# An audio tower in written program order: tanh gate, deviation by a GpSimd power, layer-norm products on ScalarE, natural order of features, 314-column streams

## The chip, the cores and the metric

The kernel runs on one core of one Trainium2 chip. The metric is the device time in microseconds (us) of one execution. TensorE (PE in the profile) does the matmuls, VectorE (DVE), ScalarE (ACT) and GpSimd (POOL) the rest, SyncE (SP) issues most transfers. Every kernel here was run beside the kernel before on the same chip.

## The reference, cut to what matters

```python
frames = pad(x).reshape(64, 157, 512)             # 64 sequences of 157 tokens
h = frames @ dct.T                                # orthonormal DCT, 512 features
x = layernorm(h)
key_phase, query_phase = tanh(x @ Wk + bk) * pi, tanh(x @ Wq + bq) * pi
V = x @ Wv + bv
total = sum over sets and planes of the causal reads of V by phase   # "scores" x V
gate = sigmoid(x @ Wg + bg)
total = gate * total + (1 - gate) * sigmoid(posw) * (reads of V by position phases)
h = h + x + total / norm @ Wo + bo
y = layernorm(h)
e = argmax(mean over tokens(y) @ Wg2 + bg2)       # one of 16 experts for each sequence
h = h + softmax gate * (y @ We[e] + be[e])
```

All is float32. Four sequences make a group, so there are 16 groups. The 157 tokens of a sequence are a tile of 128 and a tail of 29; the tails of the four sequences share one fifth tile. Every tile is normalized twice, so a group has ten layer norms.

## The kernel before

The kernel is a pipeline over groups: while TensorE does the gate and the attention of one group, the frames of the next group are transformed, normalized and transposed. The order on each engine was left to a scheduler, which may move instructions. Some names for what follows: x is a tile after the first layer norm and x2 after the second; the residual (`res`) is h + x; PSUM is the memory that TensorE writes its results to, in a few tiles that are used in turn, so that a matmul can wait for a tile to be emptied; a transpose (on TensorE, then a copy by ScalarE) turns a tile for the next matmul; folding is the sums and differences of a frame that come before its transform; phasors are the sines of the phases; the router picks the expert. The parts that matter:

```python
def layernorm(x, h):
    ...                                            # bn_stats, bn_aggr on VectorE
    nc.scalar.activation(sd, mv[:, 1:2], AF.Sqrt, bias=eps)
    nc.vector.reciprocal(rstd, sd)
    nc.vector.tensor_scalar(x, h, mv[:, 0:1], rstd, ALU.subtract, ALU.mult)

# frames: four matmuls write a PSUM tile h in runs of 128 columns
quarter = h.rearrange("p (r j) -> p r j", r=4)
...
layernorm(x, h)
nc.vector.tensor_tensor(r, h, x, ALU.add)          # residual
nc.gpsimd.tensor_tensor(r, r, bo, ALU.add)

# gate: 512 columns for the tiles, then 116 for the tails; the trace has 77 table loads of 1.28 us at the sigmoid
moving = xT[:, c, HEADS] if k == 0 else by_tail(xT[:, c, TAILS])
nc.tensor.matmul(ps[:, k, :n], wg[:, c, o * P : (o + 1) * P], moving, ...)
nc.scalar.activation(gT[:, o, :, at], pb, AF.Sigmoid, bias=bg[:, o : o + 1])

# last step of an expert; the features are put back in order by a strided view
nc.vector.scalar_tensor_tensor(o.rearrange("p (j r) -> p r j", r=4), by_r(be), gate[:, m : m + 1], by_r(h), ...)
for i in range(GB):                                # the tail tile: four stores of 29 rows
    nc.sync.dma_start(out=out[GB * g + i, P:, :], in_=o[TL * i : TL * i + LT, :])
```

## Time and profile before

| | before |
|---|---|
| median (lowest to highest) | 1661.23 us (1660.85 to 1661.28) |
| span of the profiled run | 1659.1 us |
| TensorE, VectorE, ScalarE, GpSimd busy | 96, 56, 33, 20% |
| first output projection starts | 93.4 us |
| from one group's output projection to the next, steady | 100.5 us |
| last output projection starts | 1572.0 us |
| from there to the end of the span | 87.1 us |

TensorE is busy nearly all the time, so the span is a chain of TensorE's work with short waits in it. The start of a group's output projection (the 32 matmuls of `wo`) is a good milestone: it comes once in each group, and the differences between neighbours say what a group costs. The span is then three terms: the head (until the first of these starts), 15 steps between the 16, and the end.

### The profile page before, as it was taken

The page shows a single profiled execution, that of the slowest core. Times are in us where ns is not written, and L with a number is a line of the kernel's source. Part 1 is how long each engine was busy: PE and PEld are TensorE (multiplying, and loading weights), DVE is VectorE, ACT ScalarE, POOL GpSimd, SP SyncE. Part 2 cuts the span into 40 slices and gives each one's busy share as a digit, 9 for nine tenths or more (in the row PEclk, how much of TensorE's full clock was granted, in tenths as well). Part 3 has the DMA queues.
Part 4 walks back from the last instruction along what each step waited for, and adds up shares of the span by engine and source line. Part 5 has one row for each costly group of instructions (what it writes and reads, how often), then busy time and mean ns, then how long its engine had stood idle before and what let it go on. Part 6 is the DMA issues. An engine that isn't in the chain of part 4 may idle for free. (4 is left out here: it accounts for less than half of the span.)

```text
span 1659.1 us, 18042 instructions
## 1 busy us (share of the span) xinstructions
PE 1592.7 (96%) x6724; PEld 875.5 (53%) x6724; DVE 937.4 (56%) x2162; ACT 545.1 (33%) x769; POOL 326.6 (20%) x377
## 2 busy tenths in 40 slices
PE   7999999999999999999999999999999999999984
PEld 4555556464554645556454554645546455564531
DVE  6556647466463755747466474755637556464452
ACT  3634143251522515134250432515224251342110
POOL 3203112031120403103031120312104031030102
PEclk9999999999999999999999999999999999999997
DMA  5104113141211413013141121413114130121314
GB/s 188 32 1 146 31 56 110 51 146 45 104 48 51 146 48 136 25 45 140 51 146 36 64 97 51 146 45 116 36 51 146 49 136 18 36 112 51 114 50 164
DMA packets 41206, 135.40 MB, mean 82 GB/s; under 512 B 6224, under 2 KB 6624, under 8 KB 32544
## 3 DMA queue, kind: packets, MB, share of 16 engines
q0 software_dynamic: 15616, 88.09, 15.3%
q1 hardware_dynamic: 25504, 46.17, 8.2%
q8 instruction: 53, 0.87, 0.2%
q14 instruction: 33, 0.27, 0.0%
HBM read 113.67 MB, written 20.58 MB: 81 GB/s over the span
## 5 line engine op out<-in xcount | busy, mean ns | idle before, releaser
L306 PE MATMUL mm<-xT,wg 128*128 128x512 f32 (+1 forms) x1024 | 299.9, 438 | 10.0 <-DVE res L157 9.1
L131 PE MATMUL mm<-wv,xT 128*128 128x512 f32 x640 | 283.9, 598 | 3.6 <-ACT xT L111 3.6
L131 PE MATMUL mm<-we,x2T 128*128 128x512 f32 x512 | 225.2, 598 | 10.9 <-DMA we<-in_we,rows 10.9
L131 PE MATMUL mm<-wo,tT 128*128 128x512 f32 x512 | 222.3, 592 | 0.0
L306 PEld LDWEIGHTS mm<-xT,wg 128*128 128x128 f32 x1024 | 156.3, 192 | 114.0 <-issue 92.2
L131 PEld LDWEIGHTS mm<-wv,xT 128*128 128x128 f32 x640 | 119.4, 191 | 142.5 <-issue 137.2
L101 ACT ACT_TABLE_LOAD x93 | 119.3, 1283 | 215.7 <-DVE mv L99 213.5
L131 PEld LDWEIGHTS mm<-we,x2T 128*128 128x128 f32 x512 | 98.2, 192 | 134.3 <-issue 116.3
L119 POOL TENSOR_TENSOR odd<-frame 128x256 f32<-128x256 f32 x80 | 61.3, 767 | 501.2 <-issue 491.9
L131 PEld LDWEIGHTS mm<-wo,tT 128*128 128x128 f32 x512 | 97.3, 190 | 117.2 <-issue 111.0
L453 POOL DMA_INDIRECT be<-in_be,expi x80 | 76.4, 955 | 412.8 <-DVE o L476 404.8
L174 DVE TENSOR_TENSOR v<-mm,bv 128x512 f32<-128x512 f32 x80 | 55.4, 692 | 174.9 <-PE mm L131 174.9
L345 PE MATMUL mm<-att,v 128*128 128x314 f32 x512 | 149.1, 434 | 2.3
L111 ACT COPY x2T<-tr 128x512 f32<-128x512 f32 x80 | 43.7, 588 | 260.0 <-PE tr L110 243.5
L158 POOL TENSOR_TENSOR res<-res,bo 128x512 f32<-128x512 f32 x80 | 101.5, 1278 | 137.1 <-DVE res L157 121.6
L473 DVE TENSOR_TENSOR be<-mm,be 128x512 f32<-128x512 f32 x80 | 55.3, 692 | 126.2 <-PE mm L131 75.4
L101 ACT ACTIVATE sd<-mv,eps 128x1 f32<-128x1 f32 x160 | 47.2, 295 | 207.5 <-DVE mv L99 205.5
L345 PEld LDWEIGHTS mm<-att,v 128*128 128x128 f32 x512 | 92.5, 190 | 39.5 <-DVE att L326 5.7
L110 PE MATMUL tr<-ident,x 128*128 128x128 f32 x640 | 93.4, 277 | 16.4 <-DVE x L104 15.5
L110 PEld LDWEIGHTS tr<-ident,x 128*128 128x128 f32 x640 | 73.8, 141 | 59.1 <-DVE x L104 24.2
L311 ACT ACT_TABLE_LOAD x77 | 98.8, 1283 | 1.3
L476 DVE SCALAR_TENSOR_TENSOR o<-be,gate,res 128x512 f32<-128x512 f32 x80 | 92.9, 1162 | 4.8 <-DMA out<-o 2.0
(105 smaller groups left out, 1793.8 us busy)
## 6 DMA issues: line engine op xcount, KB each, us to landing
frame<-in_frames SPq DMA_DIRECT2D x80, 256.0 KB
out<-o SPq DMA_DIRECT2D x64, 256.0 KB
out<-o SPq DMA_DIRECT2D x64, 58.0 KB
be<-in_be,expi POOLq DMA_INDIRECT x80, 4.1
wv<-in_wv SPq DMA_DIRECT2D x1, 1024.0 KB
wg<-in_wg SPq DMA_DIRECT2D x1, 1024.0 KB
wo<-in_wo SPq DMA_DIRECT2D x1, 1024.0 KB
we<-in_we,rows POOLq DMA_INDIRECT x64, 8.7
```

The source lines that it names most:

```text
L101: nc.scalar.activation(sd, mv[:, 1:2], AF.Sqrt, bias=eps)
L110: nc.tensor.transpose(tr[:, c * P : (c + 1) * P], x[:, c * P : (c + 1) * P], ident)
L119: nc.gpsimd.tensor_tensor(odd, ft[:, :2, :], ft[:, 2:, :], ALU.subtract)
L131: nc.tensor.matmul(ps, lhs(c), w[:, c, :], start=(c == 0), stop=(c == C - 1))
L158: nc.gpsimd.tensor_tensor(r, r, bo, ALU.add)
L174: nc.vector.tensor_tensor(vt, ps, bv, ALU.add)
L306: nc.tensor.matmul(ps[:, k, :n], wg[:, c, o * P : (o + 1) * P], moving, start=(c == 0), stop=(c == C - 1))
L311: nc.scalar.activation(gT[:, o, :, at], pb, AF.Sigmoid, bias=bg[:, o : o + 1])
L345: nc.tensor.matmul(ps[:, c, : 2 * L], v[i][:, cols], att[i % 2], start=True, stop=True)
L453: nc.gpsimd.indirect_dma_start(out=be, out_offset=None, in_=a["be"], in_offset=bass.IndirectOffsetOnAxis(ap=expi[:, m : m + 1], axis=0),)
L473: nc.vector.tensor_tensor(be, ps, be, ALU.add)
L476: nc.vector.scalar_tensor_tensor(o.rearrange("p (j r) -> p r j", r=4), by_r(be), gate[:, m : m + 1], by_r(h), ALU.mult, ALU.add)
```

## The change

The intent: fewer and shorter streams on TensorE, no changes of ScalarE's tables within a stage (the trace before has 222 table loads of 1283 ns), work taken from VectorE, and an order in which each layer norm stands behind TensorE's work. (The gate's sigmoid becomes a tanh, since sigmoid(z) = (1 + tanh(z/2))/2; the sum with 1 and the half are put into the scores and the mask.) The core of the diff (most of it is the same work cut into functions that are then called in order):

```diff
+    ctx.enter_context(tc.manual_schedule())           # every engine in program order
...
-        nc.scalar.activation(sd, mv[:, 1:2], AF.Sqrt, bias=eps)
-        nc.vector.reciprocal(rstd, sd)
-        nc.vector.tensor_scalar(x, h, mv[:, 0:1], rstd, ALU.subtract, ALU.mult)
+        nc.gpsimd.tensor_scalar(rstd, mv[:, 1:2], EPS, None, ALU.add)
+        nc.gpsimd.tensor_tensor(rstd, rstd, power, ALU.pow)          # power = -0.5
+        nc.gpsimd.tensor_scalar(shift, mv[:, 0:1], rstd, -1.0, ALU.mult, ALU.mult)
...
+        nc.scalar.activation(x, h, AF.Identity, bias=shift, scale=rstd)
+        nc.scalar.activation(r, h, AF.Identity, bias=shift, scale=rstd1)   # x + h in one step
...
-            quarter = h.rearrange("p (r j) -> p r j", r=4)
+        by_r = h.rearrange("p (j r) -> p r j", r=4)   # natural order: every fourth column
...
-    moving = xT[:, c, HEADS] if k == 0 else by_tail(xT[:, c, TAILS])  # 512, then 116 columns
-    nc.scalar.activation(gT[:, o, :, at], pb, AF.Sigmoid, bias=bg[:, o : o + 1])
+    s["xT"][:, c, 2 * k : 2 * k + 2, :L]              # two sequences, 314 columns, twice
+    nc.scalar.activation(to, by_halves(ps), AF.Tanh, bias=hbg[:, o : o + 1], scale=0.5)
...
-                    nc.sync.dma_start(out=out[GB * g + i, P:, :], in_=o[TL * i : TL * i + LT, :])
+                for lo, hi in ((0, TL // 2), (TL // 2, LT)):            # 16 and 13 rows
+                    nc.sync.dma_start(out=out[GB * g + i, P + lo : P + hi, :], in_=o[TL * i + lo : TL * i + hi, :])
...
+    for g in range(NG):                               # the order, as written
+        project(g); route(g - 1); phasors(g); ...     # (calls put on one line here)
+        for m in range(NM):
+            embed(g + 1, m); turn(g + 1, m - 1); embed_ln(g + 1, m); load_frame(g + 2, m)
+            gate_part(g, m); scores(...)              # four gate parts, five frame tiles
+        read(g, 0); read_tails(g); turn(g + 1, NM - 1)
+        read(g, 1) ... read(g, 3); output(g, m) ...; expert(g - 1, m) ...
+        turn_x2(g)
```

## The prediction

> **What bounds the kernel now.** I read the page first, then the timeline of TensorE in one steady group of four sequences, then the end of the program, then the waits.
>
> ```profile
> span 1659.1 us, 18042 instructions
> PE 1592.7 (96%) x6724; PEld 875.5 (53%) x6724; DVE 937.4 (56%) x2162; ACT 545.1 (33%) x769; POOL 326.6 (20%) x377
> PE   7999999999999999999999999999999999999984
> ```
>
> TensorE is the bound from the second slice to the last but two; no other engine is above 56%. So only two things change the time: how long TensorE must stream, and the short gaps in its stream. The mean durations of the groups are no measure of streaming, because matmuls overlap: I take start to start in the timeline.
>
> ```profile
> 211.88 1.02 PE L284 MATMUL mm<-xT,wkq 128*128 128x512 f32 x2
> ...
> 243.73 4.57 PE L306 MATMUL mm<-xT,wg 128*128 128x512 f32 x16 [0.64 <-DVE res L157]
> ...
> 262.89 0.66 PE L110 MATMUL tr<-ident,x 128*128 128x128 f32 x4 [0.90 <-DVE x L104]
> ...
> 263.61 1.05 PE L306 MATMUL mm<-xT,wg 128*128 128x116 f32 x8
> 264.49 0.71 PE L325 MATMUL tr<-qf,kf 128*128 128x157 f32 x4
> ...
> 271.60 5.45 PE L345 MATMUL mm<-att,v 128*128 128x314 f32 x20
> 276.88 13.90 PE L131 MATMUL mm<-wo,tT 128*128 128x512 f32 x32
> 290.61 3.60 PE L131 MATMUL mm<-wo,tT_t 128*128 128x512 f32 x8
> ```
>
> An f32 matmul is two records. One of 512 columns takes (290.61-276.88)/32 = 0.429 us, of 314 columns (276.88-271.60)/20 = 0.264, of 116 columns (264.49-263.61)/8 = 0.110. In the same way from the same view: 256 columns 0.217, 128 columns 0.110, 157 columns 0.134, 232 columns 0.196. The next groups' first projection starts 100.5 us later each (it stands at 412.89 two groups on), and the window of 100.5 us from 200 and the one after it agree to 0.02 us in TensorE's busy time.
>
> One group's stream: 112 records of 512 columns in values, output and experts 48.05; gate 32 x 0.429 + 32 x 0.110 = 17.25; key and query projection 8 x 0.429 + 8 x 0.110 = 4.31; attention reads 32 x 0.264 + 8 x 0.196 = 10.02; frames 20 x 0.110 + 20 x 0.217 = 6.54; transposes 40 x 0.109 = 4.36; scores 1.29; packed tail expert 3.57; router 1.31 + 0.23. Sum 96.9. So a group of 100.5 has 3.6 us of gaps: about 0.8 + 0.9 to 1.1 where a transpose or a gate matmul waits for a layer norm (the two waits marked above), the rest in waits for scores and in hiccups of 0.1.
>
> The end is the other place:
>
> ```profile
> 1607.67 1.07 ACT L111 COPY x2T<-tr 128x512 f32<-128x512 f32 x2 [16.30 <-PE mm L131]
> ...
> 1623.48 16.80 PE L131 MATMUL mm<-we,x2T 128*128 128x512 f32 x32 [10.95 <-DMA we<-in_we,rows]
> ...
> 1640.21 3.64 PE L465 MATMUL mm<-we,x2T 128*32 128x512 f32 x32
> ...
> 1646.27 1.41 SPq L483 DMA_DIRECT2D out<-o  x4
> ```
>
> TensorE stands 10.95 us for the last group's expert weights, because the scheduler put the old group's four experts ahead of the last routing. The last stores are issued at 1646.27 and the span ends at 1659.1: 12.8 us for four stores of 29 rows.
>
> [...]the trace has 1278 ns for res+bo against VectorE's 692.
>
> **The change, part by part.**
> 1. Narrow streams. Gate 64 x 0.264 = 16.90 (was 17.25), projections 16 x 0.264 = 4.22 (was 4.31), router in one 157-column pass, 8 packed quartets x 0.134 = 1.07 (was 1.31). That is 0.7 a group, 11 us in all.
> 2. Layer norm. Sqrt, reciprocal and VectorE's normalization (808 and 546 ns) go; VectorE keeps statistics 0.69 + 0.18. GpSimd makes three small dependent instructions (its 128x1 memsets take 0.1 us; with hand-over I estimate 0.3 each, 0.9 together), then ScalarE makes x from PSUM (0.69, as its 512-column gate). The chain from frames to x is 0.1 + 0.87 + 0.2 + 0.9 + 0.7, about 2.8 us, no shorter than before.
> 3. Order. What hides that chain is the new order: between the frames of tile m and its transposes stand a gate part (16 x 0.264 = 4.22), scores and the next frames (1.31), about 6 us; for the last tile the first reads and the tail reads, 3.7 us. So both layer-norm waits should vanish, and the scores' wait too, as they are made long before their reads.
> 4. A new gap: the five transposes of x2 now stand alone, with two PSUM banks. The trace shows that very situation at the end: copies start at 1607.67, and the fifth transpose 2 us later, so that five transposes take about 3.1 us instead of 2.2. That is 0.9 a group.
> 5. Table loads fall from 222 to 35 (counted in the built program), 187 x 1.28 = 240 us of ScalarE. VectorE loses some 150 us (normalizations, residual, reciprocals, and the strided last step of 1162 ns, which I put at 0.74). Neither is on the path.
>
> Steady group: 96.9 - 0.7 + 0.9 + 0.6 of hiccups = 97.7, that is 2.8 less than 100.5. Over the thirteen steady steps and two lighter ones (no experts in the first, no frames in the last), 12.5 x 2.8 = 35 us.
>
> Head: the setup of the position phases now stands after all values in VectorE's order, and TensorE's next matmul needs its sine: about 0.7 for the last value, some twenty small instructions 4, sine 0.5, so 5 us of standing; the first group's foldings add 3 to 4. Against this the first group's gaps before (about 7 us between 50 and 82 us) and a start some 1 us earlier go. Sum: 0.
>
> End: from the start of the last output projection (1572.0) to TensorE's last matmul were 71.9 us. After: 17.2 output, 3.6 tail expert, 3.8 transposes with the last copy, 1.1 router, 3.4 + 0.3 first expert and spread, 10.3 three experts, 13.7 four experts, 3.6 tail: 57. The routing now ends 3 us after the first old expert, since it no longer waits for the softmax; the weights then need about 6.5 us (rows to first matmul before: 1617.0 to 1623.5), and 10.5 us of experts cover it. I keep 1 us for a remaining wait: 58, so 14 less. The eight stores in place of four: issues 8 x 0.35 = 2.8[...], closing 1.3, so 6 instead of 12.8; with the contiguous last step and no wait for the bias 1 more: 8 less. End: 22 us.
>
> Sum: 1661.2 - 35 - 0 - 22 = 1604. In-order programs show stalls that such hand tracing misses, so I add 4: 1608.
>
> **The rivals.**
> - *PSUM stride.* The frames' matmuls now write every fourth column. Frames are 6.54 us a group, 105 us in all; doubled, the time would be about 1710. [...] I give it 15%.
> - *GpSimd becomes the late one.* If the power takes 2 us, the chain grows to 4.6 us and exceeds the 3.7 us of the last tile, though not the 6 us of the others: 1 us a group, 1624. Also its queue is in order: res+bo (1.28) and weight gathers (0.96 each) stand before norms. Against it: by my order there are 2 us to spare everywhere.
> - *The scheduler's freedom was worth more.* The old order filled the x2 transposes with projections; if the new order has two or three more such places of 0.9 us, a group stays at 100 and only the end is won: 1635 to 1640.
>
> **Range and chances.** The end's 22 us are nearly sure within 6, streams within 3; the groups' 35 may be 10 to 40. That gives 1592 to 1640. Under 1628 needs only end, streams and a third of the gaps: 0.78. Within 2%: 0.11. Slower by over 2% comes from the PSUM stride alone: 0.11.
>
> **What would show it.** Right: output projections start 97 to 98.5 us apart; the frames' records still 0.110 and 0.217 us start to start; no transposes waiting for x in the gate stage; x2's copies the largest steady wait; no 11 us wait for weights; under 8 us from the last store to the end. Wrong: records of frames over 0.2 us (stride), transposes released by ScalarE's x after a late GpSimd (power), or TensorE waiting in the head for more than 10 us for the sine.

The sum for the stores came to 6 us. Of it are 2.8 us of issues (four took 1.41 before) and 1.3 of closing (in the kernel before the transfers end at about 1657.8 and the span at 1659.1, by the windows view). The rest was an estimate, and that eight smaller stores land sooner than four was not shown before e5 below.

The program has 16 matmuls of `wo` on the four tiles of a group, and the trace 32 records; a record's mean duration is 592 ns, with starts 429 ns apart. VectorE's last step took 1162 ns before and 751 in the changed kernel (0.74 us was an estimate; a product of the same size on contiguous rows took 692 ns in the trace before). The 4 us for stalls were a margin; the changed kernel's trace has waits of 0.89 and 0.73 us in each group that the sum had not.

## The result

The changed kernel is correct and takes 1638.22 us (1637.75 to 1638.86, four runs) against 1661.09 us for the kernel before in the same rounds. The ratio is 0.9863, with a 95% interval of 0.9846 to 0.988. The gain is 23 us, where 53 were predicted.

| term | before | after | predicted | measured |
|---|---|---|---|---|
| head: start of the first output projection | 93.4 | 104.4 | 0 | +11.1 |
| 15 steps to the last one | 1478.6 | 1467.4 | -35 | -11.3 |
| of these: first step | 83.0 | 86.3 | | +3.2 |
| of these: 13 steady steps | 1306.2 | 1291.3 | | -14.9 |
| of these: last step | 89.4 | 89.8 | | +0.4 |
| end: from there to the end of the span | 87.1 | 65.3 | -22 | -21.8 |
| sum | 1659.1 | 1637.1 | -57, put at -53 | -22.0 |

(The head's times vary from execution to execution: another kernel with the same head, e5 below, starts its first output projection at 101.7 and its second at 189.4, where this one has 104.4 and 190.7.) So the end is as predicted, and all that is missing lies in the head (11 us) and in the steps (24 us).

The page of the changed kernel. The last line is the granted TensorE clock in tenths, in 40 slices:

```profile
span 1637.1 us, 17495 instructions
PE 1582.5 (97%) x6212; PEld 918.7 (56%) x6212; DVE 723.2 (44%) x1810; ACT 431.4 (26%) x614; POOL 509.5 (31%) x939
PEclk9899999999999999999999999999999999999999
```

VectorE and ScalarE lost 214 and 114 us and GpSimd gained 183, but TensorE is the bound, and its waits have to be looked at one by one. The second slice has a lower clock: it is the stretch around 50 us, in the head.

**The steady group.** The timeline of TensorE and its releasers at the start of a group (start, us, engine, line, operation; in brackets the idle time before it and what ended it):

```profile
325.93 1.15 PE L152 MATMUL tr<-ident,x 128*128 128x128 f32 x8 [0.24 <-ACT x2T L158]
327.26 0.66 PE L152 MATMUL tr<-ident,x 128*128 128x128 f32 x4 [0.18 <-ACT x2T L158]
327.75 2.28 PE L329 MATMUL mm<-xT,wkq 128*128 128x314 f32 x8
330.07 0.52 ACT L336 ACTIVATE u<-mm,bkq 128x314 f32<-128x314 f32 x1 [1.53 <-PE mm L329]
330.65 1.59 PE L329 MATMUL mm<-xT,wkq 128*128 128x314 f32 x5 [0.61 <-ACT u L336]
```

The five transposes of x2 wait for copies, as predicted. What was not predicted stands below them: the second half of the projection waits 0.61 us for the tanh of its first half. The kernel before had the same tanh between the two parts of its projection (512 columns, then 128), but its scheduler had put the router's matmuls and two records of the values there, and the transposes of x2 among the matmuls of the first part:

```profile
314.11 1.02 PE L284 MATMUL mm<-xT,wkq 128*128 128x512 f32 x2
314.97 0.60 PE L110 MATMUL tr<-ident,x 128*128 128x128 f32 x4
315.40 1.88 PE L284 MATMUL mm<-xT,wkq 128*128 128x512 f32 x4
317.22 1.37 PE L388 MATMUL tr<-x2T,rwg 128*32 128x128 f32 x64
318.52 1.12 PE L131 MATMUL mm<-wv,xT 128*128 128x512 f32 x2
319.48 1.08 PE L284 MATMUL mm<-xT,wkq 128*128 128x128 f32 x8
```

In the changed kernel, from start to start over a group, the transposes lose 0.74 us and the projection 0.89.

The tail of the same stage, where the last of the five tiles is normalized:

```profile
377.92 0.70 DVE L139 BATCH_NORM_STATS2 st<-mm 128x6 f32<-128x512 f32 x1 [5.06 <-PE mm L188]
379.23 0.57 POOL L144 TENSOR_TENSOR rstd<-rstd,power 128x1 f32<-128x1 f32 x1
380.19 0.78 ACT L198 ACTIVATE x<-mm,shift,rstd 128x512 f32<-128x512 f32 x1 [1.25 <-POOL shift L146]
380.64 2.10 PE L408 MATMUL mm<-att_t,v 128*128 128x232 f32 x8 [0.21 <-DVE tT L384]
380.87 0.77 ACT L200 ACTIVATE res<-mm,shift,rstd 128x512 f32<-128x512 f32 x1
381.69 0.69 PEld L408 LDWEIGHTS mm<-att_t,v 128*128 128x128 f32 x4 [0.39 <-ACT res L200]
```

The chain from frames to x is 3.1 us (377.9 to 381.0), and no transpose waits for it. But the PSUM tile that holds the frames is read by ScalarE a second time, for the residual, and becomes free only at 381.64. The reads of the tails need a PSUM tile, and TensorE loses 0.73 us in this stage.

**The head.** TensorE between the last value and the second group's first frames:

```profile
49.64 0.89 PE L308 MATMUL tr<-pf 16*128 16x157 f32 x2 [4.86 <-ACT pf L282]
52.73 0.76 PE L311 MATMUL tr<-pf_t 16*128 16x128 f32 x2 [2.21 <-DVE pf_t L298]
53.43 4.42 PE L329 MATMUL mm<-xT,wkq 128*128 128x314 f32 x8
58.47 2.38 PE L329 MATMUL mm<-xT,wkq 128*128 128x314 f32 x8 [0.61 <-ACT u L336]
64.45 1.22 PE L186 MATMUL mm<-dct_e,frame 128*128 128x128 f32 x4 [3.61 <-DVE frame L100]
```

It stands 4.86 us for the sine of the set-up, 2.21 for the copies of its result, and 3.61 for the folding of the second group's frames. The two halves of the projection are the same eight matmuls, and the first takes 4.42 us where the second takes 2.38. The windows view shows why (the third number from the end is the granted clock):

```profile
53.40:57.90 4.50, 4.45 (x9) 2.52 (x8) 0.34 (x1) 0.01 (x1) 0.00 (x0) 0.53 0.00 0
58.40:60.90 2.50, 2.38 (x8) 1.43 (x8) 0.00 (x0) 0.03 (x2) 0.00 (x0) 1.00 0.02 7
```

After the stand TensorE ran at about half its clock: the granted clock was 0.53 in the first window against 1.00 in the second. It had been 0.69 from 46.0 to 49.6 us, in the stand for the sine, and 0.50 from 49.6 to 53.4.

**The end.** The last stores, issued 1.7 us after TensorE's last matmul (1629.9):

```profile
1631.67 3.23 SPq L549 DMA_DIRECT2D out<-o  x8
```

The 11 us wait for the last expert weights is gone, and from the issue of the last stores to the end of the span there are 5.4 us, where there were 12.8.

### The profile page after: what moved, and what is told of

It reads as the page before. It is cut to its first block, busy times and chain, and to the rows that moved or that the text cites. A ratio compares the mean times of both kernels' runs of the same rounds, so it can differ in the third digit from the quotient of the medians.

```text
span 1637.1 us, 17495 instructions
## 1 busy us (share of the span) xinstructions
PE 1582.5 (97%) x6212; PEld 918.7 (56%) x6212; DVE 723.2 (44%) x1810; ACT 431.4 (26%) x614; POOL 509.5 (31%) x939
## 3 DMA queue, kind: packets, MB, share of 16 engines
q0 software_dynamic: 15616, 88.09, 15.2%
## 4 chain that ended last, share of the span: by engine, by line
PE 88%; ACT 2%; DVE 1%; issue 1%; DMA 0%; POOL 0%; DVEq 0%; POOLq 0%
PE mm L171 44%; PE mm L358 15%; PE mm L395 7%; PE mm L329 4%; PE tr L152 4%; PE mm L188 4%; PE mm L532 3%; PE mm L186 2%; PE mm L408 2%; PE tr L445 1%; ACT x2T L158 1%; PE tr L370 1%; ACT u L336 0%; DVE tT L383 0%; DVE tT L384 0%
## 5 line engine op out<-in xcount | busy, mean ns | idle before, releaser
L358 PE MATMUL mm<-xT,wg 128*128 128x314 f32 x1024 | 281.5, 427 | 0.0
L171 PE MATMUL mm<-wv,xT 128*128 128x512 f32 x512 | 229.9, 601 | 2.7 <-ACT xT L158 2.7
L358 PEld LDWEIGHTS mm<-xT,wg 128*128 128x128 f32 x1024 | 189.4, 189 | 69.9 <-issue 0.7
L171 PEld LDWEIGHTS mm<-wo,tT 128*128 128x128 f32 x512 | 97.3, 190 | 117.2 <-issue 114.8
L429 ACT ACTIVATE x<-res,shift,rstd 128x512 f32<-128x512 f32 x80 | 65.1, 813 | 359.9 <-POOL shift L146 359.9
L93 POOL TENSOR_TENSOR frame<-frame 128x256 f32<-128x256 f32 x80 | 58.4, 737 | 305.4 <-DVE even L92 284.8
L143 POOL TENSOR_SCALAR rstd<-mv 128x1 f32<-128x1 f32 x160 | 35.2, 220 | 339.2 <-DVE mv L141 338.1
L198 ACT ACTIVATE x<-mm,shift,rstd 128x512 f32<-128x512 f32 x80 | 62.2, 777 | 269.1 <-POOL shift L146 258.9
L426 DVE TENSOR_TENSOR res<-mm,res 128x512 f32<-128x512 f32 x80 | 55.3, 692 | 150.5 <-PE mm L171 150.5
L152 PE MATMUL tr<-ident,x 128*128 128x128 f32 x640 | 95.9, 282 | 11.9 <-ACT x2T L158 9.9
L139 DVE BATCH_NORM_STATS2 st<-mm 128x6 f32<-128x512 f32 x80 | 55.9, 699 | 106.1 <-PE mm L188 106.1
L144 POOL TENSOR_TENSOR rstd<-rstd,power 128x1 f32<-128x1 f32 x160 | 90.4, 565 | 13.3
```

What stands on the lines that cost most here:

```text
L93: nc.gpsimd.tensor_tensor(ft[:, :2, :], ft[:, :2, :], ft[:, 2:, :], ALU.subtract)
L144: nc.gpsimd.tensor_tensor(rstd, rstd, power, ALU.pow)
L152: nc.tensor.transpose(tr[:, c * P : (c + 1) * P], x[:, c * P : (c + 1) * P], ident)
L171: nc.tensor.matmul(ps, lhs(c), w[:, c, :], start=(c == 0), stop=(c == C - 1))
L198: nc.scalar.activation(x, h, AF.Identity, bias=shift, scale=rstd)
L358: nc.tensor.matmul(ps[:, k, : 2 * L], wg[:, c, o * P : (o + 1) * P], s["xT"][:, c, 2 * k : 2 * k + 2, :L], start=(c == 0), stop=(c == C - 1),)
```

## The experiments

My theory after the result: the new operations do what they should, and the written order gives back some 14 us at the head and 1.6 us in each group at two places that a scheduler would have filled. The main rival: these waits hide one another, so that taking one away uncovers the next; then the new operations are worth little. Twelve kernels were run, with three rounds each. All were correct. "Changed" means the changed kernel, 1638.2 us.

### Tanh of the projection after both halves (e1_whole_tanh)

```diff
         for k in range(2):
             for c in range(C): ...
-            nc.scalar.activation(u[:, 2 * k : 2 * k + 2, :], by_halves(ps)[:, k], AF.Tanh, bias=bkq)
+        nc.scalar.activation(u.rearrange("p (k b) t -> p k b t", k=2), by_halves(ps), AF.Tanh, bias=bkq)
```

> The changed kernel with one edit: the projection's tanh is one instruction after both halves, so the second half's matmuls no longer wait for the first half's tanh. My theory: in each of the 15 later groups the trace shows 0.78 + 0.11 us of that wait, and it sits on the path; output projections should start 98.4 us apart instead of 99.33 and the time be 1638.2 - 14 = 1624 (1622 to 1627). Rival: the wait is only where ScalarE's backlog from the x2 copies shows, and the same microsecond comes back at the router or at the phasors: 1635 to 1640.

Measured: 1623.19 us, ratio 0.9771 (0.9755 to 0.9787). Groups are 98.45 us apart instead of 99.33. That is 0.88 us, the size of the wait, and nothing else took its place.

### The set-up among the first group's tiles, first try (e2_setup_early)

```diff
+    first(0); first(1)
+    (gate bias, set weights)
+    first(2)
+    (turns, sine, copies of the phases)
+    first(3)
+    (key and query rows of the phases)
+    first(4)
-    (all of it behind the last value)
```

> The changed kernel with the setup of the position phases moved among the first group's values, in three pieces, its own scratch tiles, and the four copies that the second phase matmul needs put first. My theory: the 5.0 us wait for the sine, the 2.2 us wait for the copies, and the half clock that follows the standing (about 2 us in the projection) go: 1638.2 - 9 = 1629 (1626 to 1632), the first output projection at about 95 us instead of 104.4. Rival: VectorE has no room among the values, the foldings and layer norms are pushed back by the same amount and TensorE waits there: 1635 to 1640.

Measured: 1635.24 us, ratio 0.9841 (0.9824 to 0.9857). That is the rival's figure. By the medians 3 us were won, which is not clear of noise: the interval overlaps that of the changed kernel (0.9846 to 0.988). The trace shows that the wait had moved:

```profile
31.44 5.26 PE L171 MATMUL mm<-wv,xT 128*128 128x512 f32 x6 [4.42 <-ACT xT L158]
```

The sine now stood in ScalarE's queue ahead of a copy that TensorE needs, and small instructions of the set-up on VectorE ahead of the sine (eight in a row, from 27.0 to 30.4 us). On an engine that works in order, whatever is put early is put ahead of something.

### The x2 transposes mixed with the projection (e3_interleave)

```diff
         for k in range(2):
+            if x2_of is not None:
+                turn_x2(x2_of, (2 * k, 2 * k + 1))
             ...                                       # half of the projection
+        if x2_of is not None:
+            turn_x2(x2_of, (GB,))
...
-            turn_x2(g)                                # all five behind the experts
```

> The changed kernel with the five x2 transposes laid between the halves of the next group's projection (two, half, two, half, one), as the scheduler had them in the kernel before; the tanh stays one for each half. My theory: this hides both the 0.74 us of standing transposes and the 0.89 us of the projection's second half in each of 15 groups: 1.6 a group, 1638.2 - 23 = 1615 (1611 to 1620), groups 97.8 us apart. Rival: ScalarE must still do five copies and two tanh in a row, and the router and phasors then wait for it: half of it or less, 1626 to 1636.

Measured: 1619.93 us, ratio 0.9752 (0.9736 to 0.9768), groups 98.29 us apart. Both waits of the group's start went, and one came, in the list of waits (us in total, times, longest):

```profile
PE tr L450 <- ACT x2T L160: 10.8, 16, 0.7
```

The router comes right behind the fifth transpose and waits 0.7 us for its copy. (Here the expectation misread the old order: in the lines of the kernel before that are shown above, half of the first part of the projection stands between the fifth transpose and the router, and covers that copy.)

### The last frames before the fourth gate part (e4_embed_early)

```diff
+            if ahead and m == GB - 1:
+                embed(g + 1, GB); embed_ln(g + 1, GB); load_frame(g + 2, GB)
             if m < GB:
                 gate_part(g, m)
```

> The changed kernel with the last tile's frames put before the fourth gate part instead of after it, so that its layer norm is done before the reads. My theory: the 0.73 us in the tail reads come from the PSUM tile that the last layer norm still holds and from VectorE's late start on the reads (its statistics stand just before them), so most of it goes: 0.5 to 0.7 in each of 15 groups, 1638.2 - 9 = 1629 (1627 to 1631.5). Rival: VectorE's own pace in the tail reads (4 x 0.56 against TensorE's 1.57 us) is the limit, whatever stands before: 1636 to 1640.

Measured: 1639.34 us, ratio 0.9873 (0.9856 to 0.9889), groups 99.35 us apart. There was no gain, and the rival's figure came. The trace names the reason:

```profile
473.96 1.26 POOL L201 TENSOR_TENSOR res<-res,bo 128x512 f32<-128x512 f32 x1 [1.39 <-ACT res L200]
475.61 0.57 POOL L144 TENSOR_TENSOR rstd<-rstd,power 128x1 f32<-128x1 f32 x1
...
478.08 1.32 PE L395 MATMUL mm<-att,v 128*128 128x314 f32 x4 [0.49 <-ACT res L200]
```

GpSimd works in order, and the addition of a bias to the residual of the fourth tile (1.26 us, not needed for long) stood ahead of the norm of the fifth. So the PSUM tile was as late as before.

### The norm first on GpSimd (e9_norm_first)

The same as the last, and the addition behind the norm:

```diff
-        nc.gpsimd.tensor_tensor(r, r, bo, ALU.add)
+        if m != GB - 1 or g == 0:
+            add_bo(g, m)
...
             if ahead and m == GB - 1:
                 embed(g + 1, GB); embed_ln(g + 1, GB)
+                add_bo(g + 1, GB - 1)                 # the fourth tile's, behind the fifth's norm
```

> The second try at the tail's reads. As in the first try the last frame tile of the next group is embedded before the fourth part of the attention's read, and now GpSimd's addition of the bias to the residual of the fourth tile stands behind the last tile's norm, not ahead of it. My theory (the reads wait 0.7 us in each group for the PSUM tile that the last tile's norm holds): the wait goes, groups follow each other at 98.6 to 98.9 us instead of 99.33, and the time is 1629 us (1626 to 1633). Rival (the tile is freed by ScalarE's two evictions of 0.8 us, whose order against the other work is what counts, and any earlier embedding moves the wait to another read): 1636 to 1641 us.

Measured: 1626.7 us, ratio 0.9793 (0.9777 to 0.9809), groups 98.59 us apart: 0.74 us less, the whole loss of the tail's reads. One instruction of 1.26 us in the wrong place on an engine that is 31% busy cost 0.74 us in every group (e4 against this run).

### The set-up, second try (e8_setup_spread)

```diff
+    first(0); first(1)
+    (gate bias, set weights)
+    first(2)
+    (turns)
+    first(3)
+    (sine)
+    first(4)
+    (copies)
     (last value)
     (two matmuls of the phases)
```

> The second try at the head. The set-up's pieces are spread between the first group's tiles so that none stands ahead of a copy that TensorE waits for: folding matrices after the second tile, turns after the third, sine after the fourth, the copies of it after the fifth, their matmuls behind the last value. My theory (the 5.0 us for the sine, 1 to 2 us for the copies and the half clock that follows such a stand are order and nothing else): the first projection starts 8 to 10 us sooner than the 53.4 us of the changed kernel, and the time is 1629 us (1626 to 1632). Rival, as the first try at this suggested (the first group is bound by its loads and by the chain of its last tile, so that what is taken out of one wait stands again in the next): 1634 to 1638 us.

Measured: 1632.44 us (1631.28 to 1633.06), ratio 0.9829 (0.9813 to 0.9846). The first projection starts at 48.4 us in place of 53.4. So 5.8 us were won, between the two theories. Two matmuls of the phases no longer wait, but TensorE's line of the fourth tile shows the rest:

```profile
37.11 5.40 PE L171 MATMUL mm<-wv,xT 128*128 128x512 f32 x8 [2.31 <-ACT xT L158]
```

The sine, with its table load of 1.28 us, still stands ahead of one copy, the values behind that wait take 5.40 us where they take 3.70 in the tile before, and the folding of the second group's frames is as late as ever (a stand of 3.60 us).

### The tail stored whole (e5_one_store)

```diff
-                for lo, hi in ((0, TL // 2), (TL // 2, LT)):
+                for lo, hi in ((0, LT),):
```

> The changed kernel, with the output tiles of the last group stored whole (29 rows in one transfer) as in the kernel before, instead of in two pieces of 16 and 13 rows. My theory, which put about 6 us of the shorter end down to the split: the last store is again over 8 us longer from its issue to its landing, TensorE ends where it did (about 1629.9 us into the span), and the time is 1644 us (1642 to 1647) against 1638.2. Rival: the end grew shorter because the order of the last tiles let the store begin sooner, and the split does nothing: 1638 to 1639 us.

Measured: 1646.52 us, ratio 0.9917 (0.9901 to 0.9934), which is 8.3 us more than the changed kernel. The last stores:

```profile
1630.71 1.42 SPq L549 DMA_DIRECT2D out<-o  x4
```

They are issued a little sooner than the eight of the changed kernel, and the span ends 12.8 us later, at 1643.5, just as in the kernel before. So the split alone is worth 7.4 us of the end. The windows view shows what the split changes. In the kernel before, whose tails are stored whole too, from 1647.3 to 1657.3 us the 16 DMA engines are busy for 7% of their time, about one of them, and in the changed kernel for 27% from 1632.1 to 1636.1.

### The same program, reordered by the scheduler (e6_scheduler)

```diff
-    ctx.enter_context(tc.manual_schedule())
```

> The changed kernel's program without its order: the tile scheduler may reorder instructions on each engine, as in the kernel before; every operation, shape and engine stays as the change made it. Its order, seen before this run, mixes the transposes of the residual with the next projection again and puts the work of the set-up among the values. My theory (the new operations and the tail are worth 45 us or so, and the written order gives back half of it: about 14 us at the head, and 1.6 us for each group in two waits of the projection): 1612 us (1603 to 1622). Rival (the written order is what saves the 23 us, by keeping the norms and the last group's tail in place): 1645 us or more.

Measured: 1668.96 us (1667.51 to 1670.75), ratio 1.0053 (1.0036 to 1.0069). My theory missed this by 57 us, and the rival's figure came. Part of it was right: the head is 8.6 us shorter than in the changed kernel (first output projection at 95.9 us). But 11 of the 13 steady groups are 102 to 103.9 us apart (the others 104.2 and 98.3). The longest of TensorE's waits in the list (us in total, times, longest), and then the timeline of the tail's reads in one group:

```profile
PE tr L151 <- ACT x L197: 30.4, 17, 3.8
```

```profile
586.82 0.29 DVE L99 TENSOR_TENSOR frame<-even 128x128 f32<-128x128 f32 x1 [3.28 <-POOL frame L92]
587.03 0.48 DVE L383 TENSOR_TENSOR tT<-mm,tT 128x314 f32<-128x314 f32 x1
587.65 2.69 PE L394 MATMUL mm<-att,v 128*128 128x314 f32 x9 [1.29 <-DVE tT L383]
```

In the scheduler's order transposes wait for their norms (the row of the list). And VectorE stands 3.28 us with a folding of the next frames that waits for GpSimd, while the product that empties a PSUM tile of the reads stands behind it, and TensorE waits for that product. The order that a scheduler finds depends on the program it is given: the old program left TensorE 1.7 us idle in a group (100.50 less 98.81 busy in the windows view), this one 4.0 (102.80 less 98.83, from 590.0 to 692.8). So the new operations bring no gain in sum in the scheduler's order, and the written order is worth 31 us of the same instructions. But not all of the gain hangs on it: the end, from the last output projection, is 64.4 us here, so its 22 us came without the written order too, and the 15 steps are 28 us longer than in the kernel before. Not run: the old operations in a written order. How much of the gain they would have had is open; e11 below answers for one of them.

### Sqrt and reciprocal again, in the written order (e7_sqrt)

```diff
-        nc.gpsimd.tensor_scalar(rstd, mv[:, 1:2], EPS, None, ALU.add)
-        nc.gpsimd.tensor_tensor(rstd, rstd, power, ALU.pow)
+        nc.scalar.activation(sd, mv[:, 1:2], AF.Sqrt, bias=eps)
+        nc.vector.reciprocal(rstd, sd)
```

> The changed kernel, with the deviation of every norm by a Sqrt of ScalarE and a reciprocal of VectorE, as before, in place of GpSimd's add and power; all else, the order included, stays. The Sqrt brings its table loads back among the tanh and the exponentials. Theory A (in this order the norms lie beside TensorE's work except at the tail's last tile and the first group, so the chain's length is nearly free): 1638 to 1650 us. Theory B (table loads and ScalarE's in-order queue now sit ahead of copies that TensorE waits for, 2 or more of 1.28 us in each group on its path): 1655 to 1690 us.

Measured: 1670.88 us (1665.14 to 1673.42), ratio 1.0058 (1.0034 to 1.0081): 33 us more. Theory B's figure came, by a way that neither had named. The stretch of the tail's last tile:

```profile
383.06 1.28 ACT L146 ACT_TABLE_LOAD   x1
384.68 0.17 DVE L147 RECIPROCAL rstd<-sd 128x1 f32<-128x1 f32 x1 [2.16 <-ACT sd L146]
384.76 0.47 DVE L386 TENSOR_TENSOR tT<-mm,gT 128x314 f32<-128x314 f32 x1
...
385.89 1.38 PE L411 MATMUL mm<-att_t,v 128*128 128x232 f32 x5 [1.77 <-DVE tT L387]
```

VectorE stands 2.16 us with its reciprocal until ScalarE has loaded a table and made the root. Behind the reciprocal, in order, stand the products that empty the reads' PSUM tiles, and TensorE waits for those. The power on GpSimd takes that round trip out of VectorE's queue. In seven of the 13 steady steps this costs 1.43 us (100.76 us apart), in six 3.1 us or a little more (102.44 to 102.74). In the one of those that was looked at the clock fell as well: from 892.0 to 896.5 us, behind such a wait, the granted clock is 0.62, and behind the wait of an earlier group (388.2 to 394.0) it is 1.00. Both waits are 1.77 us long (before 891.37 and 385.89), so what decides stays open. I put the 3.1 us down to the wait's 1.43 and about 1.7 of slower clock, and so some 10 of the 33 us to the clock (six times 1.7, my estimate from these distances, if the other five are alike).

### The normalized tile on VectorE (e12_x_on_vector)

```diff
-        nc.scalar.activation(x, h, AF.Identity, bias=shift, scale=rstd)
+        nc.vector.tensor_scalar(x, h, rstd, shift, ALU.mult, ALU.add)
```

> The changed kernel, with the normalized tile made by VectorE, as before, and the residual still by ScalarE: the part of the change that gives the norm's products to ScalarE, half undone. Theory A (the tail's reads wait because ScalarE reads the PSUM tile twice, one after the other; with VectorE making one of the two beside it the tile is free 0.7 us sooner): 1629 us (1626 to 1634), groups at 98.6 to 99.0 us. Theory B (VectorE has the products of the reads in the same stretch, in order, so the product stands in its queue and the wait stays or grows; ScalarE is the right place): 1638 to 1650 us.

Measured: 1656.81 us (1654.54 to 1658.19), ratio 0.9971 (0.9954 to 0.9987), groups 100.42 us apart. Theory A falls, and B's direction is right though its range was too small. The tail's last tile:

```profile
586.77 0.81 DVE L198 TENSOR_SCALAR x<-mm,rstd,shift 128x512 f32<-128x512 f32 x1 [1.37 <-POOL shift L146]
587.50 0.48 DVE L383 TENSOR_TENSOR tT<-mm,gT 128x314 f32<-128x314 f32 x1
587.68 0.78 ACT L200 ACTIVATE res<-mm,shift,rstd 128x512 f32<-128x512 f32 x1 [2.17 <-DVE x L198]
588.51 1.83 PE L408 MATMUL mm<-att_t,v 128*128 128x232 f32 x8 [1.51 <-ACT res L200]
```

Two things are to be seen. VectorE waits for GpSimd's shift with the reads' products behind it, much as in the last experiment. And ScalarE's reading does not lie beside VectorE's, as theory A had it: it begins when that one ends. 586.77 + 0.81 = 587.58, and ScalarE starts at 587.68, released by VectorE's x; all nine such readings in two stretches (360 to 385 and 560 to 590 us) are released so. Why was not shown. The two paths to TensorE end almost together (ScalarE's at 588.46, VectorE's second product at 588.50), so the trace does not say which of the two alone would have cost how much.

### All repairs together (e10_all)

The set-up spread, the norm first, and the transposes mixed so that the fifth stands in the middle of the second half of the projection:

```diff
+                if x2_of is not None and x2_of > 0 and k == 1 and c == 2:
+                    turn_x2(x2_of, (GB,))
...
+    fold_once(1, 0); fold_once(1, 1); fold_twice(1, 0)   # second group's folds, ahead of the first projection
```

> All of it in one kernel: the set-up spread in the first group and the second group's first folds ahead of the first projection; the transposes of the residual mixed with the next projection so that the fifth stands in the middle of its second half; the tail's norm first. If the parts add up (about 9 us of head, 1.6 us a group of projection waits over 15 groups, 0.5 us a group of reads): 1596 us (1590 to 1604), groups at 97.2 to 97.6 us. Rival (the waits hide one another, each one removed uncovers the next, and the earlier interleaving is all there is to have): 1612 to 1620 us.

Measured: 1594.09 us (1593.13 to 1595.01), ratio 0.9598 (0.9582 to 0.9615). This beats both kernels: 44 us less than the changed one, 66 less than the kernel before. Groups are 96.80 us apart. The windows view of one group (length, then busy time of PE, PEld, DVE, ACT and POOL):

```profile
861.90:958.70 96.80, 96.80 (x389) 57.19 (x388) 44.64 (x111) 26.48 (x38) 31.79 (x59) 1.00 0.25 84
```

TensorE is busy for all 96.80 us: no wait shows in a steady group any more. The parts add up: 1.04 us for the mixing (e3), 0.7 for the router's wait (10.8 us over 16), 0.74 for the norm (e9) make 2.5, and 99.33 - 2.5 = 96.8. So the rival, that the waits hide one another, is out for the steady group. In the head it has some truth: the stand of 3.6 us for the folds is gone, but in its place transposes wait once for 4.6 us, and the second group's output projection starts at 181.1 us, still 4.7 us later than in the kernel before.

### All repairs, with Sqrt and reciprocal (e11_all_sqrt)

The edit is that of e7_sqrt, on the kernel with all repairs.

> The kernel with all the repairs of the order (1594 us), with the Sqrt of ScalarE and the reciprocal of VectorE in place of GpSimd's power. In the changed kernel as it stands the same exchange cost 33 us, all but 6 of it as a longer wait of the tail's reads. My theory (the power earns this only because the last tile's norm has no cover there; where the order gives it a gate part of 4.2 us more, the longer chain with its table loads lies beside TensorE's work): 1594 to 1602 us, groups at 96.8 to 97.2 us. Rival (the table loads stand in ScalarE's order before copies that TensorE waits for, whatever the order, so the power is worth 1.5 us or more in each group): 1615 to 1630 us.

Measured: 1611.75 us (1609.55 to 1612.41), ratio 0.97 (0.9683 to 0.9716). That is 17.7 us more than with the power, between the two theories. Groups are 97.87 us apart, 1.07 more, of which 0.94 is one wait. It is at another place than in e7:

```profile
PE mm L433 <- ACT gT L391: 10.9, 14, 0.8
```

With cover for the last norm, VectorE's stand no longer matters, but the table loads hold up ScalarE's next job:

```profile
565.26 1.28 ACT L391 ACT_TABLE_LOAD   x1
566.55 0.79 ACT L391 ACTIVATE gT<-mm,hbg 128x628 f32<-128x628 f32 x1
```

ScalarE had loaded a table for the Sqrt and now loads another for the tanh of the last gate part, and that tanh empties a PSUM tile that the reads need. So nearly half of what the power was worth in the changed kernel is order (with the clock's part, above), and the rest stays. It also says what the power is not: with Sqrt and reciprocal back, 49 of the 66 us by which the kernel with all repairs beats the kernel before remain.

## Why the prediction was wrong in size

**Right.** The streams: step 1 put their saving at 0.7 us a group. From start to start, with all waits of over 0.06 us taken out, a steady group is 97.3 us of stream in the kernel before and 96.5 in the changed one, 0.8 less. The end: 22 us predicted, 21.8 measured, in the parts as predicted. From the last output projection to TensorE's last matmul it went from 71.9 to 58.1 us (13.8, predicted 14), and from there to the end from 15.2 to 7.2 (8, predicted 8); e5 shows that the split of the stores is 7.4 of these. Step 2's chain of 2.8 us measured 3.1, and GpSimd's power 0.57 us (its addition on 128x1 0.22, its multiplication 0.27). The rival of the PSUM stride is out: the frames' records start 0.111 and 0.216 us apart (medians over the steady groups), as before. So is the rival of a late GpSimd in its first form, since a power took 0.57 us and not 2; its second form, the addition ahead of a norm in GpSimd's queue, is what e4 met.

**Wrong: the steady group.** The step was "Steady group: 96.9 - 0.7 + 0.9 + 0.6 of hiccups = 97.7". Measured: 99.33. The "0.6 of hiccups" was the term that failed. It held no wait of the projection for its own tanh (0.89 us: shown by e1, where exactly that went) and none of the tail's reads (0.73 us: shown by e9, where exactly that went). 97.7 + 0.89 + 0.73 = 99.3. That the sum closes so well is in part luck: the stream is 96.5 where the step has 96.9 - 0.7 = 96.2, the x2 transposes lose 0.75 and not 0.9, and the other small waits are 0.4 and not 0.6. So a steady step won 1.15 us and not 2.8, and thirteen of them 14.9 us. (The product 12.5 x 2.8 is a slip besides: thirteen steps alone would be 36.4.) Both waits were in reach. For the first I looked at waits that the kernel before shows, and its scheduler had hidden this one. For the second I followed x to its transposes, which is what had waited before; I did not follow the PSUM tile to the second reading that frees it.

**Wrong: the head.** The step was "Sum: 0". Measured: +11.1, and 3.2 more in the first step. The 5 us for the sine was right (4.86), and so was 3 to 4 for the foldings (3.61). Not in the sum were the copies behind the sine (2.21) and the slower clock after the stands (granted 0.53 from 53.4 to 57.9 us, about 2 us in the projection alone, 4.42 against 2.38; and 0.57 from 64.4 to 68.4, after the stand for the folds). In the first step it was that x2's last transposes wait 3.56 us, since the first group has no experts beside which the norm could lie, and a slower clock again (granted 0.72 from 127 to 131 us). What was set against all this did not come to the full: the last value ends at 44.8 us, no sooner than before (44.2), and new losses stand where the gaps of the old head were. The tries on the head alone gave 3.0 and 5.8 us, and in the kernel with all repairs the second output projection starts 9.6 of the 14.3 us sooner (181.1 against 190.7). The last 4.7, in which first loads, first norms and foldings follow one another, stay open.

**Half right: the table loads.** The prediction has them and VectorE's lost work as "Neither is on the path". In the kernel before this fits the one wait for x that was looked at (the transposes at 262.89): ScalarE's root was done at 260.24 and VectorE's reciprocal began only at 261.57. In the new order it is not so: putting Sqrt and reciprocal back cost 33 us (e7), and 18 where the order covers the norm (e11). I had counted 240 us of ScalarE's time and called it free, and the right question was what stands behind a wait in the same queue.

**The third rival** ("The scheduler's freedom was worth more", 1635 to 1640 us) has the time right by luck and the reason half right. It had the end alone won and the groups unchanged; in fact the 15 steps won 11.3 us and the head, which it does not mention, lost 11.1. Two of the "two or three more such places of 0.9 us" exist (0.89 and 0.73). But the scheduler's freedom was worth less than nothing for this program (e6, 1669 us): what was worth more is another written order (e10, 1594 us).

## What to carry to other kernels

When engines work in order, ask of each wait on a helper engine what stands behind it in that engine's queue, and of each PSUM tile what its last reader is; a helper that is a third busy can hold up the bound engine in every round (GpSimd here, 31% busy, for 0.74 us). A wait that the old kernel does not show may be one that its order hid, so list the waits that the code contains, not only those that the trace has. When a new order gives less than was hoped for, do not undo it: read where the bound engine stands, and move one instruction at a time, as here, where a handful of moves brought the gain from 23 us to 66.
